# A gated cross-attention and mixture-of-experts layer: the products with V moved in front of the scores of the second and third steps

## The chip, the cores and the metric

The kernel runs on one core of a Trainium2 chip. The metric is the device time of one execution in microseconds (us). The five engines of the core each work through an instruction list of their own, in order, and wait for each other by semaphores: PE (TensorE, matrix products into PSUM; PEld is its weight load), DVE (VectorE), ACT (ScalarE), POOL (GpSimd) and SP (SyncE, which here only issues DMAs).

## The reference, cut to what matters

```
B, L, D = 4, 1024, 256; 64 context rows; 16 heads of 64; 8 experts, F = 1024, top 2
qh = layernorm(x) @ w_qs;  kh = ctx @ w_ks;  vh = ctx @ w_vs
attn = softmax(qh . kh)                         # over the 64 context rows
out  = (attn . vh) * qh                         # gated by the query itself
x    = x + tanh(g_xattn) * (out @ w_proj.T + b_proj)
logits = layernorm(x) @ gate_w.T;  combine = softmax over the two best experts
y    = sum over the chosen experts of combine * (silu(layernorm(x) @ w1[e]) @ w2[e])
x    = x + tanh(g_ffn) * y
```

All of it is in float32.

## The kernel before, in words

The 4096 rows are cut into NG = 8 groups of 512, and each group into T = 4 tiles of 128 rows. Two groups make one batch row (GB = 2).

The attention is a software pipeline over rounds g = 0 to 8, each with steps t = 0 to 3 (the loop at L1330 to L1378). In step t of round g these are recorded, in this order:

- `probabilities` (L420): the scores of tile t for all 16 heads, 16 records on PE into one wide PSUM tile `sc` (L424), and then the softmax. Its chain is DVE maximum (`mx`, L433), DVE difference (`pr`, L435), ACT exponential (L438), DVE sum (`sm`, L440), DVE reciprocal (L441) and POOL product (L443). The tag `pr` has two buffers.
- `transpose_probabilities` (L448) for the tile of the step before: eight transposes on PE (`pa`, L454), which wait for the POOL product, and two ACT copies into `aT` (L455).
- `attend` (L459), the products with V, for the group of the round before (g - 1). One call does eight heads: two sets of four products of 64 x 64 x 512 (`po`, L469), each set into two PSUM banks, and each bank is then taken by a DVE product with the queries (L478, 128 x 512), which writes the gated result into `qT`. In the kernel before both halves stand in step 1: the first behind the transposes, the second in `finish` (L1263), behind the step's queries.
- `queries` (L404) for the next group, spread over the steps by `parts`: four pairs of heads in step 0, two in step 1, one in step 2 and one in step 3, in the middle rounds. Round 1 has one pair in step 1. Round 7 has none, since there is no group 8. A pair is the PE product `pq` (L408) and an ACT copy (L416).
- `project` (L480) in steps 2 and 3, for group g - 1: PE products `pp` (L486), which read all of `qT` and so wait for the L478 products.
- `after` (L1278): routing of the two groups that are done, in the odd rounds 3, 5 and 7 from step 0 to 3. Its step 1 normalises the first of them (`ln_norm`: four DVE operations L312 in place, each recorded behind the newest softmax's reciprocal by `behind_sums`, then PE transposes `pt_b` L317 and ACT copies L323), and multiplies it with the gate weights (`logits`: PE `pl` L508, DVE copy `lT` L516, PE transpose `pl_t` L518, DVE copy L520). Its step 2 does the same with the second group.

The experts are worked off in slots of 256 rows (`run_slots`, a generator). A piece of it, that is one `next(slots)`, is some products of the first layer (`ph`, L955, with ACT Silu L963) or of the second (`py`, L1183). `pieces` says how many stand in each step of rounds 6, 7 and 8. Before the change they stand at the end of the step.

Most PSUM results of the attention (`pa`, `pq`, `po`, `pt`, `pl`, `pp`, and the slots' tiles before round 8) share one pool, `ps1`, of four banks in turn: a product can't start before the consumer of the tile four places earlier has read it. The scores use `ps2`, two wide tiles in turn.

The order in which the program records work isn't yet the order on the engines. A scheduler lists each engine's instructions by what it expects to be ready first. It may move later work ahead of earlier, except where an instruction is pinned or put behind another. The list it makes is fixed before the kernel runs.

Of the kernel before, what the change touches and what calls it, by code (L numbers as in the profile page):

```python
# [21 lines left out]
def kernel(  # L22
# [40 lines left out]
    H, _, DK = w_qs.shape  # L63
    E, _, F = w1.shape
# [3 lines left out]
    NG = B * L // G  # L68
    GB = L // G
    NP = H // 2  # L70
# [35 lines left out]
    def bank(name, spare=False):  # L106

        if spare:
            return ps2.tile([P, 2, 512], F32, tag="ps2", name=name)[:, 0]
        return ps1.tile([P, 512], F32, tag="ps1", name=name)  # L110
# [53 lines left out]
    wk, _ = next(load_wk)  # L164
# [84 lines left out]
    def apart(tensor, dma, part=None, behind=()):  # L249

        writers = [writer for name in behind for writer in written[name]]
        tc.declare_no_dep(dma.ins, group=tensor, keep=writers, reason="different rows")
        tc.add_to_no_dep_group(tensor, dma.ins)
        for writer in writers:
            tc.add_manual_dep(
                dma.ins,
                writer.name,
                mybir.DependencyInfo(mybir.DependencyClass.Sync, mybir.DependencyReason.DATA),
                reason="rows of the part",
            )  # L260
        if part:
            written.setdefault(part, []).append(dma.ins)
# [62 lines left out]
    def add_bias(g):  # L325
        nc.gpsimd.tensor_tensor(
            xg[g], xg[g], bias.unsqueeze(1).to_broadcast([P, T, D]), ALU.add
        )
# [68 lines left out]
    def halves(name, share="group"):  # L397

        return [block([P, NP // 2, G], f"{name}_{i}", share) for i in range(2)]

    def of_pair(t, p):
        return t[p // (NP // 2)][:, p % (NP // 2), :]
# [45 lines left out]
    def transpose_probabilities(g, t, pr, aT):  # L448
        prv = pr.rearrange("p (i j) m -> p i (j m)", j=2)
        n = 512 // P  # L450
        for p0 in range(0, NP, n):
            pt = bank(f"pa_{g}_{t}_{p0}")
            for i in range(n):
                nc.tensor.transpose(pt[:, i * P : (i + 1) * P], prv[:, p0 + i, :], ident)  # L454
            nc.scalar.copy(  # L455
                aT[p0 // n][:, :, t * P : (t + 1) * P], pt.rearrange("p (i q) -> p i q", i=n)
            )

    def attend(g, pairs, qT, aT):  # L459

        for q in range(pairs[0] // 2, pairs[-1] // 2 + 1):


            po = [bank(f"po_{g}_{2 * q + j}") for j in range(2)]
            for r in range(2):
                for j in range(2):
                    half = slice(j * M, (j + 1) * M)
                    i = q * 2 + r
                    nc.tensor.matmul(  # L469
                        po[j][r * DK : (r + 1) * DK],  # L470
                        vs[half, g // GB, i, :],
                        of_pair(aT, i)[half],
                        start=True,
                        stop=True,
                    )
            for j in range(2):
                own = of_pair(qT, 2 * q + j)
                nc.vector.tensor_tensor(own, po[j], own, ALU.mult)  # L478

    def project(g, qT, t0):  # L480

        pp = bank(f"pp_{g}_{t0}").rearrange("p (t d) -> p t d", d=D)
        for i in range(2):
            t = t0 + i
            for p in range(NP):
                nc.tensor.matmul(  # L486
                    pp[:, i, :],
                    of_pair(qT, p)[:, t * P : (t + 1) * P],
                    wp[:, p, :],
                    start=(p == 0),  # L490
                    stop=(p == NP - 1),
                )
        nc.vector.scalar_tensor_tensor(
            xg[g][:, t0 : t0 + 2, :], pp, tg[:, 0:1], xg[g][:, t0 : t0 + 2, :], ALU.mult, ALU.add
        )
# [704 lines left out]
    def run_slots(slots):  # L1200

        nonlocal in_order
        ahead = 3
        issued.clear()
        tokens, weights = {}, {}

        def load(s):
            if s in slots:
                weights[s] = load_weights(s)

        def load_next(s):
            if s in slots:
                tokens[s] = load_tokens(s)

        for s in slots[:ahead]:
            load(s)
            load_next(s)
        load_next(slots[0] + ahead)
        yield
        yield  # L1220
        xT = transposed(slots[0], tokens[slots[0]][1])
        yield
        pending = first = None
        for s in slots:
            in_order = is_wide(s)
            a, b = weights.pop(s)
            ids, xin = tokens.pop(s)
            if s == slots[-1] and pending:
                yield from combine(*pending)
                pending = None  # L1230
            for hT in hidden_by_quarters(s, xT.shape[2], first) if first else hidden(s, a, xT):
                yield
            first = None
            if s + 1 in slots:
                xT = transposed(s + 1, tokens[s + 1][1])
                if is_wide(s + 1):
                    first = first_sums(s + 1, weights[s + 1][0], xT)
                yield
            if pending:
                yield from combine(*pending)  # L1240
            pending = (s, ids, b, xin, hT, quarter_sums(s, b, hT) if by_quarters(s) else None)
            load(s + ahead)
            load_next(s + ahead + 1)
        yield from combine(*pending)
# [16 lines left out]
    held = {}  # L1261

    def finish(g, step):  # L1263

        qT, aT = held[g]
        if step == 1:
            attend(g, range(NP // 2, NP), qT, aT)
        elif step >= 2:
            project(g, qT, (step - 2) * 2)

    def leave(g):
        apart("out", nc.scalar.dma_start(of[g], xg[g]), f"out{g // HG}")
# [41 lines left out]
    slots = run_slots(range(NA + OFTEN))  # L1314
    pieces = {HG + 2: (0, 0, 1, 1), HG + 3: (3, 3, 2, 2), HG + 4: (3, 3, 3, 3)}
# [14 lines left out]
    for g in range(NG + 1):  # L1330
        attention_ends = g == NG
        if g < NG:
            qT, aT = qTs[g], halves(f"aT_{g}", "hidden" if g % 2 and g + 1 < NG else "group")
            held[g] = (qT, aT)
        for h in parts[g]:
            if h == len(qTs):
                qTs.append(halves(f"qT_{h}"))
        for t in range(T):
            if t == 0 and g >= 2:
                leave(g - 2)  # L1340
            if g < NG:
                pr = probabilities(g, t, qT)
            if last:
                transpose_probabilities(*last)

            b = (g - GB - 1) // GB
            ends, behind = b * GB + GB - 1, (g - GB - 1) % GB * T + t if b >= 0 else -1
            if behind == T:
                placing(ends)
            if g and t == 1:  # L1350
                attend(g - 1, range(NP // 2), *held[g - 1])
            for h, pairs in parts[g].items():
                queries(h, qTs[h], pairs[t])
            if 0 <= g - 1 < NG:
                finish(g - 1, t)
            last = (g, t, pr, aT) if g < NG else None
            if g == 0:
                for _ in range(value_parts[t]):
                    next(pending_values)
            if behind >= 0:  # L1360
                after(ends, behind)
            if g == 0 and t == 1:
                tc.keep_in_program_order(nc.scalar.activation(tg, tg, AF.Tanh))
                tc.keep_in_program_order(
                    nc.gpsimd.tensor_scalar(bias, bias, tg[:, 0:1], None, ALU.mult)
                )
                for h in range(2):
                    add_bias(h)
            if g + 2 < NG:
                if t == 0 and (g + 2) % GB == 0:  # L1370
                    stats = ln_stats(list(range(g + 2, g + 2 + GB)), f"a{g + 2}")
                elif t == 2:
                    ln_norm(g + 2, stats, "a")
                    add_bias(g + 2)
            if g < 2:
                clear(g * T + t, 2 * T)
            for _ in range(pieces[g][t] if g in pieces else 0):
                next(slots)  # L1378

    leave(NG - 1)  # L1380
# [6 lines left out]
    for _ in slots:  # L1387
# [3 lines left out]
    _, used = nc.values_load_multi_w_load_instructions(  # L1391
        in_use[0:1, 0:1], min_val=0, max_val=NB, bass_reorder=False
    )
# [38 lines left out]
```

## Time and profile before

| what | value |
|---|---|
| median of 13 executions | 863.18 us (861.21 to 865.07) |
| the profiled execution, own time | 865.22 us |
| its span in the profile | 863.5 us |
| PE busy | 837.0 us, 97% |
| DVE busy | 495.8 us, 57% |
| POOL busy | 266.2 us, 31% |
| ACT busy | 244.3 us, 28% |
| all products with V on PE (L469) | 33.8 us, 256 records |
| all their DVE products (L478) | 64, 0.68 us each (median) |
| mean granted TensorE clock | 0.994 |

The profile shows one execution. "Busy" is the time in which an engine works on an instruction; "idle before" is the time it stood still in front of one, with the instruction that ended the wait behind an arrow. A timeline row gives start, duration, engine, line, operation, tiles, and the number of records. In the timeline the products with V stand between 77.5 and 406.5 us, one pair of halves in each round from 1 to 8.

### The profile page before, as it was taken

How to read it: one execution, taken by the hardware profiler on the slowest of the kernel's cores; microseconds unless marked ns; L12 is line 12 of the kernel's file. 1: busy time of each engine (PE TensorE's matmuls, PEld its weight loads, DVE VectorE, ACT ScalarE, POOL GpSimd, SP SyncE). 2: the span in 40 equal slices, each digit the busy share in tenths (PEclk: the TensorE clock that was granted, in tenths of full speed). 3: DMA queues.
4: the chain of work that ended last, by engine and by line, in shares of the span. 5: the costliest groups of instructions: out<-in, count | busy, mean ns of one | idle time of the engine just before them, and what ended most of it. 6: DMA issues, size and time to landing. Idle time of an engine off the chain costs nothing. (4 is left out here: it accounts for less than half of the span.)

```text
span 863.5 us, 13306 instructions
## 1 busy us (share of the span) xinstructions
PE 837.0 (97%) x4684; PEld 681.9 (79%) x4684; DVE 495.8 (57%) x1202; ACT 244.3 (28%) x413; POOL 266.2 (31%) x216
## 2 busy tenths in 40 slices
PE   8999999999999999899999999999999999999995
PEld 6565858577675758687888888899999998899995
DVE  4466484669648885864238724656666653645520
ACT  2573242333333232541113012222222121221210
POOL 3042212213731164115523732222222232223132
PEclk9999999999999999999999999999999999999998
DMA  9999999401200043336765878776665775456611
GB/s 196 334 340 342 339 345 340 129 1 38 80 32 1 25 158 107 113 90 196 217 191 137 218 188 210 221 183 163 164 156 135 194 180 138 123 133 179 172 23 38
DMA packets 165032, 141.79 MB, mean 164 GB/s; under 512 B 72685, under 2 KB 159076, under 8 KB 161248
## 3 DMA queue, kind: packets, MB, share of 16 engines
q1 hardware_dynamic: 145456, 118.79, 47.0%
q0 software_dynamic: 12912, 17.11, 10.1%
q10 hardware_dynamic: 6592, 4.98, 1.8%
q8 instruction: 39, 0.64, 0.3%
q14 instruction: 33, 0.27, 0.1%
HBM read 78.73 MB, written 62.46 MB: 163 GB/s over the span
## 5 line engine op out<-in xcount | busy, mean ns | idle before, releaser
L1146 POOL DMA_INDIRECT out_dram<-x,ids x69 | 108.4, 1571 | 290.4 <-DVE x L1161 77.8
L1183 PE MATMUL py<-w,hT 128*128 128x256 f32 (+1 forms) x960 | 186.0, 362 | 0.0
L1183 PEld LDWEIGHTS py<-w,hT 128*128 128x128 f32 (+1 forms) x960 | 160.0, 181 | 21.6 <-issue 1.7
L955 PE MATMUL ph<-xT,w 128*128 128x256 f32 x576 | 129.5, 380 | 0.3 <-ACT hT L963 0.3
L443 POOL TENSOR_TENSOR pr<-pr,sm 128x1024 f32<-128x1024 f32 x32 | 61.4, 1918 | 209.4 <-DVE sm L441 145.0
L408 PE MATMUL pq<-nT_a,wq 128*128 128x512 f32 x256 | 116.0, 596 | 5.7 <-DVE qT L478 5.4
L955 PEld LDWEIGHTS ph<-xT,w 128*128 128x128 f32 x576 | 107.9, 190 | 15.9 <-issue 1.4
L486 PE MATMUL pp<-wp,qT 128*128 128x256 f32 x512 | 113.1, 379 | 0.0
L486 PEld LDWEIGHTS pp<-wp,qT 128*128 128x128 f32 x512 | 97.1, 190 | 18.2 <-issue 5.7
L408 PEld LDWEIGHTS pq<-nT_a,wq 128*128 128x128 f32 x256 | 46.3, 190 | 58.0 <-issue 44.2
L963 ACT ACTIVATE hT<-ph 128x1024 f32<-128x1024 f32 (+1 forms) x40 | 37.2, 939 | 173.9 <-PE ph L955 151.0
L606 POOL DMA_INDIRECT table<-x,to_row x64 | 63.0, 984 | 42.7 <-DVE x L595 24.8
L424 PEld LDWEIGHTS sc<-keys,qT 128*128 128x128 f32 x512 | 62.6, 192 | 11.2 <-issue 10.8
L424 PE MATMUL sc<-keys,qT 128*128 128x128 f32 x512 | 67.1, 278 | 0.0
L1161 DVE TENSOR_SCALAR x<-py,ids 128x256 f32<-128x256 f32 (+1 forms) x53 | 24.7, 468 | 70.5 <-PE py L1183 70.4
L455 ACT COPY aT<-pa 128x512 f32<-128x512 f32 x64 | 34.4, 591 | 82.1 <-PE pa L454 72.2
L433 DVE TENSOR_REDUCE mx<-sc 128x16 f32<-128x1024 f32 x32 | 38.9, 1217 | 28.0 <-PE sc L424 27.9
L440 DVE TENSOR_REDUCE sm<-pr 128x16 f32<-128x1024 f32 x32 | 39.0, 1218 | 23.9 <-ACT pr L438 23.8
L1019 ACT ACTIVATE hT<-hT 128x384 f32<-128x384 f32 (+1 forms) x66 | 32.9, 499 | 53.5 <-DVE hT L1016 50.5
L1005 PE MATMUL ph<-x,sa 128*128 128x192 f32 (+1 forms) x264 | 44.8, 319 | 2.3 <-issue 2.0
L416 ACT COPY qT<-pq 128x512 f32<-128x512 f32 x64 | 36.5, 580 | 36.4 <-PE pq L408 36.1
L1016 DVE TENSOR_TENSOR hT<-ph,u 128x384 f32<-128x384 f32 (+1 forms) x66 | 34.8, 528 | 15.8 <-PE ph L1005 11.8
(278 smaller groups left out, 1008.9 us busy)
## 6 DMA issues: line engine op xcount, KB each, us to landing
w<-in_L_ffn_w_dram SPq DMA_DIRECT2D x58, 1024.0 KB, 5.7
table<-empty SPq DMA_DIRECT2D x8, 5016.0 KB, 38.9
x<-table SPq DMA_DIRECT2D x116, 64.0 KB, 3.3
out_dram<-x ACTq DMA_DIRECT2D x8, 512.0 KB
x<-in_x_dram SPq DMA_DIRECT2D x7, 512.0 KB, 9.7
out_dram<-x,ids POOLq DMA_INDIRECT x69, 4.2
wq<-in_L_xattn_w_qs_dram SPq DMA_DIRECT2D x4, 256.0 KB, 5.1
wv<-in_L_xattn_w_vs_dram SPq DMA_DIRECT2D x2, 512.0 KB, 7.8
```

What stands on the lines that cost most here:

```text
L408: product = nc.tensor.matmul(pq, wq[:, c, p * P : (p + 1) * P], nT[g][:, c, :], start=(c == 0), stop=(c == NC - 1),)
L424: nc.tensor.matmul(sc[:, p // 2, :, p % 2, :], of_pair(qT, p)[:, t * P : (t + 1) * P], kT[g // GB][:, p, :], start=True, stop=True,)
L433: nc.vector.tensor_reduce(mx, scv, AX.X, ALU.max)
L440: nc.vector.tensor_reduce(sm, pr, AX.X, ALU.add)
L443: nc.gpsimd.tensor_tensor(pr, pr, sm.unsqueeze(2).to_broadcast([P, H, M]), ALU.mult).ins,
L486: nc.tensor.matmul(pp[:, i, :], of_pair(qT, p)[:, t * P : (t + 1) * P], wp[:, p, :], start=(p == 0), stop=(p == NP - 1),)
L606: nc.gpsimd.indirect_dma_start(out=table.rearrange("r (u w) -> (r u) w", w=2), out_offset=bass.IndirectOffsetOnAxis(ap=to_row[:, k, i : i ...
L955: nc.tensor.matmul(ph[:, i, :], a[:, c, f * P : (f + 1) * P], xT[:, c, :], start=(c == 0), stop=(c == NC - 1),)
L963: nc.scalar.activation(hT[f0 // per_tile][:, f1 : f1 + step, :], ph, AF.Silu)
L1005: nc.tensor.matmul(to[:, f, :], left[:, (f0 + f) * P : (f0 + f + 1) * P], right, start=not onto and f == 0, stop=True, skip_group_check=on ...
L1146: rows_added = nc.gpsimd.indirect_dma_start(out=outf.rearrange("n (h d) -> (n h) d", d=w)[:rows_of], out_offset=bass.IndirectOffsetOnAxis( ...
L1183: product = nc.tensor.matmul(py[t][i * m : (i + 1) * m], hT[f // per_tile][:, f % per_tile, t * P : t * P + m], b[:, f, i * w : (i + 1) * ...
```

## The change

The two halves of the products with V get places of their own. In rounds 1 to 7 the first half is recorded in step 1 and the second in step 2, each ahead of that step's scores. In the last round, which has no scores, the halves go to steps 0 and 1, and the step's slot pieces, which stood at its end, now stand in front of them, behind the transposes.

```diff
@@ def finish(g, step):
         qT, aT = held[g]
-        if step == 1:
-            attend(g, range(NP // 2, NP), qT, aT)
-        elif step >= 2:
+        if step >= 2:
             project(g, qT, (step - 2) * 2)
+
+    def attend_half(g, half):
+
+        attend(g, range(half * (NP // 2), (half + 1) * (NP // 2)), *held[g])
@@ for g in range(NG + 1): ... for t in range(T):
             if t == 0 and g >= 2:
                 leave(g - 2)
+            if g and g < NG and 1 <= t <= 2:
+                attend_half(g - 1, t - 1)
             if g < NG:
                 pr = probabilities(g, t, qT)
             if last:
                 transpose_probabilities(*last)
+            if g == NG:
+                for _ in range(pieces[g][t]):
+                    next(slots)
+                if t < 2:
+                    attend_half(g - 1, t)
...
-            if g and t == 1:
-                attend(g - 1, range(NP // 2), *held[g - 1])
...
-            for _ in range(pieces[g][t] if g in pieces else 0):
+            for _ in range(pieces[g][t] if g in pieces and g < NG else 0):
                 next(slots)
```

No operation is added or taken away, on any engine or queue.

## The prediction

> **What bounds the kernel now.** I read the page's busy times first, then PE's waits, then the timeline around the products with V.
>
> ```profile
> span 863.5 us, 13306 instructions
> ...
> PE 837.0 (97%) x4684; PEld 681.9 (79%) x4684; DVE 495.8 (57%) x1202; ACT 244.3 (28%) x413; POOL 266.2 (31%) x216
> ```
>
> PE is busy 97% of the span. The change leaves its work alone, so all that can change is its 26.5 us of idle time. The list of PE's waits says how much of this is around the moved products:
>
> ```profile
> PE pq L408 <- DVE qT L478: 5.4, 6, 1.6
> PE pa L454 <- POOL pr L443: 2.1, 2, 1.3
> PE pt_b L317 <- DVE qT L478: 2.0, 4, 0.7
> ...
> PE po L469 <- DVE qT L478: 0.9, 1, 0.9
> ```
>
> PE stands before the L478 products 5.4 + 2.0 + 0.9 = 8.3 us: the products with V fill the four banks and DVE, busy with the softmax, doesn't empty them in time. That is the most that better spacing can win, plus about 1 us in round 8, where both halves take 4.76 us (401.78) against two times 1.88 (from the start of one half at 126.62 to PE's next work at 128.49), and the 1.31 us wait for POOL in round 7 (350.75 below).
>
> Rounds have little else to spare: the timeline shows how long scores take to become transposable.
>
> ```profile
> 107.80 1.95 PE L424 MATMUL sc<-keys,qT 128*128 128x128 f32 x16
> ...
> 109.78 1.23 DVE L433 TENSOR_REDUCE mx<-sc 128x16 f32<-128x1024 f32 x1 [1.03 <-PE sc L424]
> ...
> 115.14 1.90 POOL L443 TENSOR_TENSOR pr<-pr,sm 128x1024 f32<-128x1024 f32 x1 [9.38 <-DVE sm L441]
> ```
>
> The scores end at 109.75 and POOL at 117.04: 7.3 us with nothing in the way.
>
> **The change part by part.** For the order on each engine I use the list built from the changed program, and durations from the trace. In the odd rounds that list does not do what the change says: the second half stands behind the third step's scores, not in front. PE slots, start to next start: `sc` 1.79, eight `pa` 0.87, one `pq` pair 1.72, one half of the products 1.88, half a `pp` 6.91, `ph` of one round-7 step 3.46. T is the start of the first half.
>
> *Rounds 1 to 6, first half.* It now runs where the scores ran, and its four L478 products (1.14 us after the start, then 2.48 us: the rows at 127.76) lie beside the scores, to T + 3.6; the scores end at T + 3.7. The stalls in front of `pq` go. But the step's softmax starts 1.9 us later against the next step's transposes: where five pieces of PE work, about 9.4 us in round 1, covered the chain, the first half is no longer among them. What is late next is POOL's product. In round 1 PE has `pa`, one `pq`, the second half and `sc` to offer; DVE also has one L478 product between sum and reciprocal. The chain ends at T + 11.75, against 86.08 - 74.78 = 11.30 now: +0.5 us.
>
> In even rounds DVE comes to step 1 late, with the row statistics (in round 2 until 119.5, while T is 117.32). There L478 and three L312 products stand in front of the maximum, which starts at T + 6.0 where the scores end at T + 3.7. The chain ends at T + 13.85; now it is 130.38 - 117.32 = 13.06: +0.8. In round 4 the statistics end 2.5 to 3.6 us after T = 211.53 (the later end, if the routing of round 3 in front of them slips by 1 us), so the chain at T + 14.2 to 15.4; now 225.00, T + 13.5. That is +0.7 to +1.9; I take +1.3, the middle. In round 6 two statistics operations move behind the table: +0.4 (0 to +0.7).
>
> In rounds 3 and 5 the scheduler also moves the second half far back: behind all of `sc_2`, most of `sc_3`, `pt_b`, `pl` and `pl_t`. The two `pq` pairs (3.4 us) and the scores fill the time until L312. In round 3 `pp` starts now at 180.12, 18.5 us after 161.62, with `sc_3` still to do (1.79). By the same addition it would start at T + 19.35 with `sc_3` done: 18.5 + 1.79 - 19.35 = 0.9 us ahead. I take -0.9 each (bounds -1.5, where all stalls go, and +0.5, where the L312 operations meet POOL's product for longer). Sum of rounds 1 to 6: 0.5 + 0.8 - 0.9 + 1.3 - 0.9 + 0.4 = **+1.2 us**, bounds -8 (every stall goes, nothing replaces it) and +4.
>
> *Round 7* decides. It has no `pq`. Now it looks so:
>
> ```profile
> 350.75 1.09 PE L454 MATMUL pa<-ident,pr 128*128 128x128 f32 x8 [1.31 <-POOL pr L443]
> ...
> 359.14 1.38 DVE L312 TENSOR_SCALAR x<-x,mv_b,rstd_b 128x256 f32<-128x256 f32 x4
> ...
> 363.49 0.28 DVE L516 COPY lT<-pl 128x128 f32<-128x128 f32 x1
> ...
> 366.33 2.95 DVE L312 TENSOR_SCALAR x<-x,mv_b,rstd_b 128x256 f32<-128x256 f32 x4
> ...
> 367.45 1.04 PE L454 MATMUL pa<-ident,pr 128*128 128x128 f32 x8
> ```
>
> In the new order PE has: first half, `sc_1`, `pa_0`, `sc_2`, `sc_3`, `pt_b`, `pl`, `pl_t`, `ph`, second half, `pa_1`. DVE has: four L478, `mx_1`, difference, a slot transpose (0.7), `mx_2`, difference, `sm_1`, `mx_3`, reciprocal, four L312, `sm_2`, reciprocal, four more L312 (the second group's), and only then L516. Add up from 347.49. The first half waits inside for the Silu of `ph` (348.40 to 349.49), which holds its banks, and ends at about 350.5; `sc_1` to 352.3; `pa_0` to 353.15, its old 1.31 us wait gone; `sc_2` to 354.95. DVE: L478 to 351.9, `mx_1` 352.45 to 353.7, difference to 355.0 (this frees the tile of `sc_3`, which then runs to 356.85), transpose 355.65, `mx_2` 356.85, difference 358.15, `sm_1` 359.4, `mx_3` 360.65, reciprocal 360.9. Four L312 beside POOL's product take 2.95 as in the row at 366.33 (one of the operations lasts up to 2.07), so 363.85; `sm_2` and reciprocal to 365.35; four L312 to 368.2; L516 to 368.5. PE thus idles from 356.85 to about 361.4, again between the `pt_b` transposes, and from 365.4 to 368.5 in front of `pl_t`. Then `ph` 3.46 and the second half 1.88: `pa_1` at 373.85, now 367.45. **+6.4 us**, bounds +3.5 (both L312 groups at 1.38, one wait hidden) and +8.
>
> A PE that idles for 4.5 us may also lose its clock. After the 1.96 us wait at 539.84 (`ph` L1005, released by "issue") the stretches read, with busy times per engine and then granted clock:
>
> ```profile
> 540.00:544.00 4.00, 2.20 (x10) 1.99 (x11) 3.84 (x9) 0.35 (x1) 1.73 (x1) 0.90 0.67 204
> 544.00:548.00 4.00, 4.00 (x19) 4.00 (x18) 1.95 (x6) 1.20 (x3) 0.00 (x0) 0.67 1.04 325
> ```
>
> At half clock, 0.90 and 0.67 of two 4 us stretches mean (0.10 + 0.33) x 4 = 1.7 us lost. One such loss: **+1.7 us**, bounds 0 (round 7's work waits for DVE anyway) and +5 (three of them). [...]
>
> *Round 8.* The halves are parted by `ph` pieces, and L478 gets time: 4.7 - 3.8 = **-0.9 us** (0 to -1). But the slot pieces are now earlier, so behind the last `pp` only one `py` (3.46 us) covers the normalisation of group 6; now `ph` and two `py` do (437.22 to 447.58). From the end of that `pp` to the end of L312 it takes 442.56 - 437.22 = 5.3 us, so PE stands about **+1.3 us** in front of `pt_b` (0 to +1.5). POOL's table writes (L606, 16 x 1.27 us) start some 14 us later; nothing reads them before the late table, so they cost nothing, and up to 1 us if a scatter queues behind them. SP's weight loads shift with the `ph` that free their buffers; the expert stage shows no PE wait for a DMA in the trace, so nothing again.
>
> Sum: 1.2 + 6.4 + 1.7 - 0.9 + 1.3 = +9.7 us. The profiled execution took 865.22, 2.0 us over the median; against it that is 874.9, against the median of 863.18 it is **872.9 us**.
>
> **Rivals.**
>
> *Faster: the stalls simply go.* The mechanism is the banks: L478 runs beside the scores and no PE work waits for it. DVE's idle time (43%) speaks for it. Against it, DVE is 9.32 us busy in the 9.55 us from 354.20 to 363.75. Its place is round 7, and its price the 8.1 us that my forecast charges there (6.4 + 1.7). It decides if L516 is done by about 365.4, when PE reaches `pl_t`: DVE would have to run its list 3 us faster than the rows add up to. PE then wins 8.3 + 0.9 us: 863.2 - 9.2 = 854; with a chain wait of 0.5 us in each of six rounds, 857.
>
> *Round 7 is milder, and the odd rounds give back.* The second L312 group isn't met by POOL and the clock holds: +3.5 + 1.2 - 0.9 + 0.5 = 867.5; with rounds 1 to 6 at -2, 864.
>
> *The cold PE spreads.* Waits of 1 to 1.5 us in even rounds drop the clock there too: 872.9 + 3 x 1.7 = 878.
>
> **Numbers.** Forecast 62%, the stalls go 12%, milder 16%, cold 10%. The range 862.5 to 879 takes in all but the first rival. A difference of 0.2% (1.7 us) is about what a measurement of this kernel can tell from none. Faster, below 861.5: 13%; same, to 864.9: 8%; slower: 79%.
>
> **What would show it.** Right: PE waits named `pt_b` <- DVE L312 and `pl_t` <- DVE L516, together 6 us or more, between the seventh round's scores and `pa`; `pq` <- L478 nearly gone; `pa` <- POOL grown to 4 us or more; a stretch of half clock after round 7. Wrong: `pl_t` not waiting there, or L516 ahead of the second L312 group.

## The result and the profile after

| kernel | median | ratio to before, 95% interval |
|---|---|---|
| before | 863.23 us (861.21 to 865.82) | |
| after | 881.09 us (877.38 to 883.22) | 1.0204 [1.0192, 1.0217] |

The change costs 2.04% of 863.2, that is 17.6 us, far more than the noise; the interval reaches from 1.92% to 2.17%, so whether the loss is above 2% is open. The forecast was 872.9 us, and the range ended at 879. The profiled execution after took 883.8 us, 2.7 over its median; that of before was 2.0 over its own.

The page of the kernel after, its span and its busy times:

```profile
span 882.1 us, 13307 instructions
...
PE 846.4 (96%) x4684; PEld 683.3 (77%) x4684; DVE 499.4 (57%) x1202; ACT 244.2 (28%) x413; POOL 265.5 (30%) x216
```

PE's busy time has grown by 9.4 us (837.0 before) although its work is the same. Some of it ran at half clock (13.7 us of round 7 at 0.50); but 5.6 us of the growth lie in rounds 1 to 6, where the clock was full (1.00 from 11.8 to 356.5 us): there PE waited inside stretches that count as busy (see the trap at the end of the section on why the prediction was wrong). Its waits in the kernel after (what it waited for; us in total, times, longest):

```profile
PE pt_b L317 <- DVE x L312: 8.9, 7, 3.6
PE pl_t L518 <- DVE lT L516: 2.9, 2, 2.0
PE pa L454 <- POOL pr L443: 2.4, 4, 0.8
PE po L469 <- ACT hT L963: 2.1, 1, 2.1
...
PE po L469 <- ACT qT L416: 1.2, 1, 1.2
```

The wait `pq` <- L478 (5.4 us before) isn't in the list any more, so the change does what it says. Waits for the normalisation, for its gate logits, for a Silu and for a copy of queries stand in its place. Most of this is in round 7. The timeline of the kernel after there:

```profile
348.11 0.71 DVE L928 STREAM_TRANSPOSE xT<-x 128x512 f32<-128x512 f32 x1 [5.49 <-DMA x<-table]
...
350.57 1.22 DVE L433 TENSOR_REDUCE mx<-sc 128x16 f32<-128x1024 f32 x1
...
356.17 2.47 PE L469 MATMUL po<-aT,vs 64*64 64x512 f32 x8 [2.14 <-ACT hT L963]
...
369.23 2.95 DVE L312 TENSOR_SCALAR x<-x,mv_b,rstd_b 128x256 f32<-128x256 f32 x4
...
369.61 0.44 PE L317 MATMUL pt_b<-ident,x 128*128 128x128 f32 x2 [3.60 <-DVE x L312]
371.58 1.54 PE L317 MATMUL pt_b<-ident,x 128*128 128x128 f32 x6 [1.54 <-DVE x L312]
...
373.50 2.95 DVE L312 TENSOR_SCALAR x<-x,mv_b,rstd_b 128x256 f32<-128x256 f32 x4
...
376.38 0.28 DVE L516 COPY lT<-pl 128x128 f32<-128x128 f32 x1
...
376.71 0.48 PE L518 MATMUL pl_t<-ident,lT 128*128 128x128 f32 x1 [1.98 <-DVE lT L516]
376.98 5.31 PE L955 MATMUL ph<-xT,w 128*128 128x256 f32 x16
```

Read from below: `ph` took 5.31 us, where 16 such records in front (349.39) took 3.62. PE waited for `pl_t`, since DVE did the second group's L312 first; before that it waited twice for the first group's L312, and before that, inside the first half, for a Silu. At the top stands a row that the prediction didn't have: DVE waited 5.49 us for a DMA and then transposed the first slot's tokens (L928), and only behind that came the maximum of step 0.

The clock in the same stretch, by the windows of the kernel after (us; busy time of PE, PEld, DVE, ACT, POOL with records; granted clock; DMA share; GB/s):

```profile
352.90:366.00 13.10, 10.88 (x73) 7.71 (x72) 8.62 (x12) 6.84 (x8) 1.90 (x1) 0.87 0.41 119
...
370.20:380.40 10.20, 6.38 (x32) 4.49 (x33) 6.61 (x11) 2.36 (x3) 3.09 (x2) 0.50 0.01 2
```

0.87 of 13.1 us is one stretch of 3.4 us at half clock (356.50 to 359.92 at 0.50); later come 10.2 us in a row at 0.50.

**Where the time is lost**, by the starts of the same block in both traces. How much later a block starts than in the trace before is called its shift below; a stretch costs what the shift grows by over it. The trace after is 0.48 us late at the transposes of round 0's last tile (68.70 before), 5.36 late at those of round 6's last tile (343.16), and 18.12 late at those of round 7's (393.03). So rounds 1 to 6 cost 4.9 us and round 7 costs 12.8.

### The profile page after: what moved, and what is told of

It is laid out like the page before. It is cut to its first block, busy times and chain, and to the rows that moved or that the text cites. A ratio compares the mean times of both kernels' runs of the same rounds, so it can differ in the third digit from the quotient of the medians.

```text
span 882.1 us, 13307 instructions
## 1 busy us (share of the span) xinstructions
PE 846.4 (96%) x4684; PEld 683.3 (77%) x4684; DVE 499.4 (57%) x1202; ACT 244.2 (28%) x413; POOL 265.5 (30%) x216
## 5 line engine op out<-in xcount | busy, mean ns | idle before, releaser
L955 PE MATMUL ph<-xT,w 128*128 128x256 f32 x576 | 131.4, 384 | 0.4 <-ACT hT L963 0.3
L606 POOL DMA_INDIRECT table<-x,to_row x64 | 63.8, 996 | 24.5 <-issue 16.1
L478 DVE TENSOR_TENSOR qT<-po,qT 128x512 f32<-128x512 f32 x64 | 40.1, 674 | 19.9 <-PE po L469 19.9
L1005 PE MATMUL ph<-x,sa 128*128 128x192 f32 (+1 forms) x264 | 45.3, 321 | 2.4 <-issue 2.0
```

What stands on the lines that cost most here:

```text
L606: nc.gpsimd.indirect_dma_start(out=table.rearrange("r (u w) -> (r u) w", w=2), out_offset=bass.IndirectOffsetOnAxis(ap=to_row[:, k, i : i ...
L955: nc.tensor.matmul(ph[:, i, :], a[:, c, f * P : (f + 1) * P], xT[:, c, :], start=(c == 0), stop=(c == NC - 1),)
L1005: nc.tensor.matmul(to[:, f, :], left[:, (f0 + f) * P : (f0 + f + 1) * P], right, start=not onto and f == 0, stop=True, skip_group_check=on ...
```

## The experiments

Each edit is told against the kernel before or after. Microseconds given for a ratio are its distance from 1, times 863.2.

**One part of the change at a time.** Only the conditions change; a half that isn't moved stays at its old place. For round 7 alone:

```diff
+            if g in (7,) and t == 1:
+                attend_half(g - 1, 0)
+            if g in (7,) and t == 2:
+                attend_half(g - 1, 1)
             if g < NG:
                 pr = probabilities(g, t, qT)
...
-            if g and t == 1:
-                attend(g - 1, range(NP // 2), *held[g - 1])
+            if g in (1, 2, 3, 4, 5, 6, 8) and t == 1:
+                attend_half(g - 1, 0)
             for h, pairs in parts[g].items():
                 queries(h, qTs[h], pairs[t])
+            if g in (1, 2, 3, 4, 5, 6, 8) and t == 1:
+                attend_half(g - 1, 1)
```

This is against the kernel before and cut to the loop. The others are the same with rounds 1 to 6, with the last round, or with only the first half of round 7.

Rounds 1 to 6:

> Only rounds 1 to 6 are changed; rounds 7 and 8 stand as before. Theory: the parts add, and the trace after shows these six rounds 4.9 us longer (shift of +0.49 us at the start of attention, +5.36 us at the end of round 6): 868.1 us, ratio 1.0057. Rival (the term of the prediction): +1.2 us, 864.4, ratio 1.0014. Rival two: what the rounds lose is only a later start that round 7 would have waited for anyway: within 1 us of before.

Measured: 870.94 us, 1.0084 [1.0069, 1.0098], +7.3 us. Above the theory's figure, and far above the prediction's. The trace says why: 4.9 us lie inside the six rounds (shift -0.92 to +3.95), as in the trace after, and **2.6 more in round 7, whose code isn't changed** (+3.95 to +6.57).

Round 7:

> Only round 7 is changed. Theory: its loss of 12.8 us (shift +5.36 us at its start, +18.12 us at the last transposes of probabilities behind it) is its own: 876.0 us, ratio 1.0148, with PE waits pt_b <- DVE L312 and pl_t <- DVE L516 and stretches of half clock behind 340 us, about 10 us or more in all. Rival (the size in the prediction, 6.4 + 1.7): 871.3 us, ratio 1.0094. Rival two: round 7 is that bad only because rounds 1 to 6 hand it a later softmax; alone it loses 6 us at most: below 869.2.

Measured: 871.84 us, 1.0093 [1.0078, 1.0109], +8.0 us. Not the theory's 12.8, but the 8.1 of the prediction. The two are not read at the same place: at the transposes of round 7's last tile this trace is 9.8 us late (shift -0.53 to +9.29), and 1.3 us come back in round 8. So 3.0 of the 12.8 come from the rounds before.

Round 8:

> Only the last round is changed: halves between slot pieces. Theory: the halves win 0.9 us, the waits for the normalisation of group 6 cost 1.8 (pt_b 0.90 and pl_t 0.90 in the trace after): +0.5 to +0.9, 863.7 to 864.1, ratio 1.0006 to 1.0010. Rival: slot pieces that run ahead cost elsewhere in the expert stage: more than +2 us. Rival two: only the gain shows, -0.9: 862.3.

Measured: 864.76 us, 1.0020 [1.0008, 1.0032], +1.7 us, above both bounds of the theory, though its interval reaches down to 0.7; by its shifts the round loses 1.7 too (-0.43 to +1.24). The waits of PE in this kernel name the second loss, which the prediction lacked:

```profile
PE pl_t L518 <- DVE lT L516: 1.5, 3, 0.8
PE pt_b L317 <- DVE x L312: 0.9, 1, 0.9
```

The 0.84 stands in round 8, in front of `pl_t` at 452.20. The 0.9 us that the halves win and these two waits leave +0.8; what makes the rest of the 1.7 the list of waits doesn't show. The three parts add up to 0.84 + 0.93 + 0.20 = 1.97%, the whole change 2.04%: inside the intervals they add.

First half of round 7 alone:

> In round 7 alone, only the first half is moved ahead of the second step's scores; the second half stays behind the transposes of step 0. Theory: the loss starts with the first half waiting for the Silu of the expert product in front of it (2.14 us in the trace after) and the later scores of step 1, which push L312 and L516 back on DVE: +5 to +8 us, 868 to 871. Rival: the loss is made by the second half, which stands behind the expert products and takes their slot: within 1.5 us of before, 862 to 865.

Measured: 865.28 us, 1.0015 [1.0000, 1.0030], +1.3 us. The theory falls: of round 7's 8.0 us the early first half makes the smaller part. By its own trace it is 3.3 us of 9.8 (shift -0.61 to +2.65). Most of the loss comes only with the second half moved too: it then stands behind `ph`, and PE has none of it to do while DVE works through its list.

**The late rows.** POOL writes the rows of a group to the table in DRAM (L606), six behind each softmax product, and the first slot reads them in round 7. The rows of the kernel with rounds 1 to 6 changed, at the start of round 7:

```profile
337.88 0.96 POOL L606 DMA_INDIRECT table<-x,to_row  x1 [0.30 <-issue]
...
346.51 0.71 DVE L928 STREAM_TRANSPOSE xT<-x 128x512 f32<-128x512 f32 x1 [5.31 <-DMA x<-table]
...
348.98 1.22 DVE L433 TENSOR_REDUCE mx<-sc 128x16 f32<-128x1024 f32 x1
...
356.28 1.09 PE L454 MATMUL pa<-ident,pr 128*128 128x128 f32 x8 [2.90 <-POOL pr L443]
```

and the same instructions of the kernel before:

```profile
332.05 0.96 POOL L606 DMA_INDIRECT table<-x,to_row  x1 [0.30 <-issue]
...
340.70 0.71 DVE L928 STREAM_TRANSPOSE xT<-x 128x512 f32<-128x512 f32 x1 [3.44 <-DMA x<-table]
...
343.45 1.22 DVE L433 TENSOR_REDUCE mx<-sc 128x16 f32<-128x1024 f32 x1
```

The kernel is 3.95 us late there; the last write is 5.8 late, L928 5.8, the maximum 5.5. The halves push the scores of round 6 back, with them the softmax products, with these the writes queued behind them on POOL, the load, the transpose, and on DVE all that stands behind it. If that is so, writing more rows behind the first product (8, 6 and 2 behind three products, not 6, 6 and 4) must win the 2.6 us back, in a round that this kernel leaves as it was:

```diff
-            first, last = min(6 * (step - 4), 2 * R), min(6 * (step - 3), 2 * R)
+            ends = (0, 8, 14, 16, 16) if g == HG - 1 else (0, 6, 12, 16, 16)
+            first, last = ends[step - 4], ends[step - 3]
```

> The kernel with rounds 1 to 6 alone changed, and in rounds 5 and 6 POOL writes the rows of the first four groups to the table as 8, 6 and 2 behind three softmax products, not 6, 6 and 4. Theory: 2.6 of the 7.7 us that those rounds cost are lost in round 7, whose code is as before: the last writes come 1.9 us later, so the tokens of the first slot land later, their transpose (L928) holds DVE, and the maximum of step 0 behind it starts 1.6 us late. With the last writes 2.5 us earlier: 868.3 us against 870.9, ratio 1.006; pa <- POOL in round 7 falls from 2.90 to about 1.3 us, and the stretch of half clock at 357.5 is gone. Rival: round 7 loses by the clock alone or by another DMA: 870.9, ratio 1.0084, and the wait for pa stays. Rival two: eight writes in a row hold the next softmax product of POOL: over 872.

Measured: 868.61 us, 1.0045 [1.0030, 1.0060]. Round 7 now costs 0.16 us (shift +5.03 to +5.19), and the mean granted clock of the profiled execution is 0.998, against 0.992 without the edit. Its rows at the start of round 7:

```profile
345.39 0.71 DVE L928 STREAM_TRANSPOSE xT<-x 128x512 f32<-128x512 f32 x1 [3.10 <-DMA x<-table]
...
355.78 1.09 PE L454 MATMUL pa<-ident,pr 128*128 128x128 f32 x8 [1.31 <-POOL pr L443]
```

The wait for `pa` is the 1.31 us of the kernel before. The late rows are shown. The same edit on the whole changed kernel:

> The changed kernel with the same 8, 6 and 2 writes. Theory: the same late rows cost it 1.6 us on DVE in round 7, and the exponential, the Silu and with it the first half of the products are as much later; one or two windows of half clock (1.7 us each) go too: 881.1 - 1.6 - 1.7 = 877.8 us, down to 876, ratio 1.015 to 1.017. Rival: in the changed order DVE is late in any case, so nothing changes: 881, ratio 1.020.

Measured: 877.10 us, 1.0158 [1.0132, 1.0184], so 4.0 us of the 17.6 are won, as the theory had it. The first half's wait for the Silu fell from 2.14 to 0.37 us. Of the theory's other term, one or two windows of half clock less (1.7 us each), at most one was won: the mean granted clock of the profiled execution is 0.988, against 0.987 without the edit. By the shifts round 7 costs 10.2 us here (+3.68 to +13.89), 2.6 less than the 12.8, which the interval allows.

**The order on DVE.** `behind_sums` puts L312 behind the newest softmax's reciprocal. Taken away for chosen groups, the scheduler sets L312 where the statistics are ready, behind the maximum of step 0. For group 4, which is normalised in round 7:

```diff
-            with behind_sums() if name == "b" else nullcontext():
+            with behind_sums() if name == "b" and g != 4 else nullcontext():
```

> The kernel with round 7 alone changed, and the normalisation of group 4 (L312) need not stand behind the reciprocal of step 1 on DVE: in the built order it stands between the maximum and the difference of step 0, and L516 in front of the second group's L312. Theory (what costs is the order of DVE's list): the waits pt_b <- L312 (3.60 + 1.55) and pl_t <- L516 (1.97) go, with them the half clock: 871.8 falls by 7 to 9 us, to 863 to 865, ratio 0.999 to 1.002. Rival (what costs is the place of the halves on PE: the wait for the Silu, the later scores): 868 or more, ratio over 1.005, with the idle time behind sc or in front of pa.

Measured: 865.59 us, 1.0012 [0.9998, 1.0027], so 7.0 of 8.0 us are gone with the place of the halves unchanged. The mean granted clock of its profiled execution is 0.996, against 0.992 with round 7 alone, and `ph` behind `pl_t` takes 3.62 us, against 5.67. Its waits of PE:

```profile
PE pa L454 <- POOL pr L443: 1.7, 2, 1.0
PE pl_t L518 <- DVE lT L516: 1.6, 1, 1.6
PE pa L454 <- DVE qT L478: 1.1, 1, 1.1
```

None is for L312 now; PE still waits 1.6 for `pl_t`. So the halves' place on PE costs round 7 little by itself. It costs together with DVE's order: either one put right, this order or the second half's place (the run with the first half alone), takes most of the loss away. The same for groups 0 and 2, with rounds 1 to 6 changed (`g not in (0, 2)`):

> The kernel with rounds 1 to 6 alone changed, and the normalisation of groups 0 and 2 (L312) in rounds 3 and 5 need not stand behind the reciprocal of step 1 on DVE. Theory: there PE waits 0.19 and 1.25 us per round for L312, which now runs beside POOL's product (2.95 us for four); ahead of the product it takes about 1.4, and nothing is late in its place: -1.5 to -2.9 us, 868 to 869.4, ratio 1.0056 to 1.0073. Rival: the softmax behind it comes 1.4 us later and pa waits instead: 870.9, ratio 1.0084.

Measured: 865.97 us, 1.0017 [1.0002, 1.0033], by the ratios 5.8 us below the run without it, twice the theory's. In the kernel with rounds 1 to 6 changed, round 3 has

```profile
171.21 2.95 DVE L312 TENSOR_SCALAR x<-x,mv_b,rstd_b 128x256 f32<-128x256 f32 x4
...
171.47 1.90 POOL L443 TENSOR_TENSOR pr<-pr,sm 128x1024 f32<-128x1024 f32 x1 [9.62 <-DVE sm L441]
...
173.57 0.76 PE L317 MATMUL pt_b<-ident,x 128*128 128x128 f32 x4 [1.25 <-DVE x L312]
```

and with L312 free

```profile
156.31 0.41 DVE L312 TENSOR_SCALAR x<-x,mv_b,rstd_b 128x256 f32<-128x256 f32 x1 [0.66 <-POOL rstd_b L295]
...
157.77 1.05 DVE L312 TENSOR_SCALAR x<-x,mv_b,rstd_b 128x256 f32<-128x256 f32 x3
...
160.71 1.90 POOL L443 TENSOR_TENSOR pr<-pr,sm 128x1024 f32<-128x1024 f32 x1 [4.44 <-DVE sm L441]
```

Away from POOL's product the four take 1.46 us, not 2.95, and start 13 to 15 us earlier. So `pt_b` no longer waits, and the second half's products also stand in a better place: `pp` of round 3 is 3.9 us earlier against before than without the mend (-1.43 and +2.47), where round 3's first transposes differ by 0.2 (+2.33 and +2.50). But this kernel still loses 4.2 us in round 7, to the late rows.

**The parts together.** With both mends (L312 freed, and more rows written early), on rounds 1 to 6:

> Rounds 1 to 6 changed, rounds 7 and 8 as before, with both mends: L312 of groups 0 and 2 need not wait for the reciprocal of step 1, and the table's rows are written 8, 6 and 2. In the run with the first mend alone, rounds 1 to 6 stood 1.7 us ahead of before at the end of round 6 (-0.48 to -2.16) and lost 4.2 in round 7. Theory: that loss is the late rows alone: 863.2 - 1.7 + 0.2 = 861.7 us, ratio 0.998. Rival: round 7 loses for another reason (the softmax of round 6 ends late): 866, ratio 1.0017 as without the rows.

Measured: 861.42 us, 0.9973 [0.9961, 0.9984]. As the theory had it: the loss in round 7 was the late rows. The control, with no half moved:

> The kernel before, all products with V in their old places; only L312 of groups 0 and 2 need not wait for the reciprocal of step 1. Theory: the gain of that mend in the changed rounds 3 and 5 needs the new places, where L312 collides with POOL's product; in the old ones the transposes pt_b wait 0.72 and 0.27 us per round for L478, and at most these go: 861.2 to 863.7, ratio 0.998 to 1.0005. Rival: the gain is the mend's alone, and the old order with it is as fast as or faster than the new: below 860, ratio under 0.996.

Measured: 861.25 us, 0.9976 [0.9964, 0.9988]. So the freed L312 alone, in the old order, wins as much as both mends with all six rounds changed: moving the halves in all of them brings nothing. Halves moved only in the rounds where that won by the shifts, 3, 5 and 6:

> Only rounds 3, 5 and 6 changed, with both mends. By the shifts of the run with L312 free, round 3 won 1.69 us, round 5 1.68 and round 6 0.85, where rounds 1, 2 and 4 lost 0.6, 0.74 and 1.8. Theory (the rounds are independent of one another): 863.2 - 4.2 + 0.2 = 859.2 us, ratio 0.9954, faster than before. Rival: what rounds 3, 5 and 6 won was time that rounds 1, 2 and 4 had lost before them: 862 to 864, ratio 0.999 to 1.001.

Measured: 858.74 us, 0.9955 [0.9938, 0.9971], **faster than both kernels**, by 0.45% against the one before. By the shifts, rounds 1 to 6 win 4.2 us here and 1.7 in the control. The two intervals of the whole time overlap, so a gain of the places beyond the freed L312 rests on the traces. The whole change with both mends, L312 free in round 7 as well:

> The changed kernel whole, with both mends, L312 of group 4 in round 7 free as well. Theory: the parts add: rounds 1 to 6 -1.7, round 7 +1.2 (the run of round 7 alone with L312 free: -1.21 to -0.04 us), round 8 +1.7 (the run of round 8 alone): 863.2 + 1.2 = 864.4 us, ratio 1.0014, so 16.7 of the 17.9 us lost are DVE's and POOL's order. Rival: they do not add, since round 7 gets a later softmax from round 6: 868 or more, ratio 1.0055.

Measured: 866.55 us, 1.0032 [1.0020, 1.0044]. Of 17.6 us lost 2.8 remain, or 5.3 against the control, which has L312 freed for groups 0 and 2. The parts add less well than the theory had it (864.4): round 7 costs 2.1 us here (shift -2.19 to -0.10), with waits for `pa` of 0.98 and 1.97 us.

## Why the prediction was wrong

The direction, the waits named for round 7 and its size were right; of the signs named, only `pa` <- POOL failed: said to grow to 4 us or more, it came to 2.4. **The step that failed is the sum of rounds 1 to 6, "+1.2 us"** (bounds -8 to +4): it measured +7.3, of which 4.9 lie in the rounds themselves and 2.6 in round 7. Rounds 3 and 5 at the wrong end of their bounds, round 4 and the late rows make up the difference.

| step | predicted | measured |
|---|---|---|
| rounds 1, 2 | +0.5, +0.8 | +0.6, +0.75 |
| rounds 3, 5 | -0.9 each | +0.5 each |
| round 4 | +1.3 | +2.5 |
| round 6 | +0.4 | -0.05 |
| late rows, paid in round 7 | nothing | +2.6 |
| round 7 itself, with its clock | 6.4 + 1.7 = +8.1 | +8.0 |
| round 8 | -0.9 + 1.3 = +0.4 | +1.7 |

The rounds are from the kernel with rounds 1 to 6 changed, by the shifts of its blocks; rounds 7 and 8 are from the runs of each alone.

- *Late rows.* The prediction followed POOL's table writes in round 8 only, and of SP's weight loads said "nothing again". In round 6 it moved the softmax product that the writes are queued behind, and did not follow the queue: POOL, then SP's load, then L928 in front of DVE's maximum. In the whole change this delay also made the Silu late: PE waited 2.14 us for it, where round 7 alone has 0.38 and the prediction had about 1.
- *Rounds 3 and 5.* The -0.9 took the stalls of L478 to go and little to come. L312 met POOL's product, as the other bound (+0.5) said, and +0.5 is what it cost.
- *Round 4.* The second half waits for a bank, and the bank for an ACT copy of queries that stands behind a table load and an exponential. In the kernel with rounds 1 to 6 changed:

```profile
221.91 1.28 ACT L438 ACT_TABLE_LOAD   x1 [1.24 <-DVE mv_b L288]
223.21 1.06 ACT L438 ACTIVATE pr<-pr 128x1024 f32<-128x1024 f32 x1
224.17 0.57 ACT L416 COPY qT<-pq 128x512 f32<-128x512 f32 x1
...
224.79 1.08 PE L469 MATMUL po<-aT,vs 64*64 64x512 f32 x6 [1.17 <-ACT qT L416]
```

From its first start to its last the second half took 3.59 us there, against 1.36 before. The prediction asked what DVE does with the banks that the products fill. It didn't ask who holds the banks that they take. Rounds 1 and 2 fit in size, but they hold such a wait too: 2.18 against 1.78 us, and 2.36 against 1.36.
- *Round 7.* Alone, the next transposes of probabilities came 8.45 us later than before (shift -0.53 to +7.92), predicted 6.4 + 1.7. The waits were 3.60 + 1.55 for L312 and 1.97 for `pl_t`, and `ph` took 2.05 us longer (5.67 against 3.62; the mean granted clock of this execution is 0.992, against 0.994 before). The prediction's reason, DVE's list, holds: with L312 free most of the loss goes.
- *Half clock.* One loss of 1.7 us was predicted. After has 13.7 us at half clock in round 7, which would be 6.8 us if PE had always had work; but in the first two thirds of its longer stretch (370.16 to 373.57 and to 376.98) PE was busy only 1.54 and 1.42 us, and waited for DVE. On the path are 1.7 us of `ph` (5.31 against 3.62), and up to 0.7 us of the scores of step 1 (2.68 against 1.95) and 0.9 us of the first half (its last eight records took 2.47, against 1.57 with round 7 alone).
- *Round 8.* The halves won the 0.9 us to the digit, and `pt_b` waited 0.90. The wait for `pl_t` behind it (0.84) is the same two-step chain through DVE as in round 7, and was left out. About 0.9 us of the 1.7 have no named cause.

Of the rivals, "the stalls simply go" failed at the place it named: L516 was not done when PE came to `pl_t`. "Round 7 is milder" failed too: both groups' L312 met POOL's product (2.95 us each), and the clock fell (to 0.50 for 13.7 us). "Cold PE spreads" was nearest in time (878) but not in cause: no clock was lost in rounds 1 to 6 (1.00 from 11.8 to 356.5 us), and so none in their even ones.

One trap in reading: the listed idle time of PE in rounds 1 to 6 is no longer with the change (7.7 us before and 6.8 after, summed over waits of 0.1 us and more), though the rounds take 4.9 us more. A record lasts longer by the trace than PE takes to the next start: 0.28 us against 0.11 for the last of a score tile, so each wait behind scores shows 0.17 us too little. Most is hidden between the products with V, whose records last 0.59 us: from one to the next in rounds 1 to 6, start to start, they took 16.7 us before and 20.7 after, and of these 4.0 us the list shows 1.2. Starts of blocks compared between two traces don't have this fault.

## What to carry to other kernels

When work on one engine is moved, write out the whole list of every engine behind it, and at each item ask who else queues there: here 12 to 15 of 17.6 us went away with the products left in their new places, once a normalisation was no longer tied to a softmax sum and fewer table writes stood behind the last softmax product. An order that was tied on purpose need not fit new places, and here it was not the best for the old ones either (the control is 0.24% faster): when the places change, loosen the ties first and then test the places, one round at a time. What a move gains on the waits that it aims at is at most their sum, while what it delays has no such limit.

## What the runs showed of the hardware

**The clock before and after.** In both traces the granted clock was 1.00 or 0.50, and within a trace its changes lie whole multiples of 3.413 us apart. What follows is by stretches of that length, without the first and the last 12 us. Before the change the one fall (at 543.21) followed a stretch in which PE was busy 1.45 of 3.41 us. After it the falls at 356.50, 370.16 and 561.30 followed 1.27, 0.44 and 1.45 us. The least busy stretches at full clock that no fall followed have 1.8 us before (311.11) and 1.97 after (172.18). Before, the wait of 1.62 us in front of `pq` at 313.20 was not followed by half clock; after, those of 2.14 and 3.60 us in round 7 were. The wait of 1.96 us in front of `ph` (L1005) is in both traces, and one stretch of 3.413 us at 0.50 followed it in each. Two traces make no rule: the kernel with the last round alone changed has this wait too (2.0 us), and the mean granted clock of its profiled execution is 0.998, against 0.994 before.

**How it came back.** From 370.2 to 380.4 us after the change the clock stood at 0.50 for three such stretches, with PE busy 1.54, 1.42 and 3.41 us in them; behind the third it was full again. The other stretches at half clock in the two traces, again without the first and the last 12 us, had PE busy 3.39 us or more (543.21 before, 356.50 and 561.30 after), and each was followed by full clock.

**DVE and POOL side by side.** Four L312 operations took 1.46 us without POOL's product beside them (the run with rounds 1 to 6 changed and L312 free) and 2.95 with it (the run without the mend), while the product took 1.90 in both cases. One of the four has the difference: in the kernel after, at 172.86, it took 2.06 us, where the other three took 0.33 to 0.40, and ended 0.15 us behind the product. What held it is not shown: by the trace it started 0.01 us ahead of the product.
